# Attention in phases of two slots: six PSUM banks, waits bank by bank

## The chip, the cores and the metric

The kernel runs on one core of one Trainium2 chip. The time is the device time of an execution in microseconds. TensorE (PE) multiplies matrices, and its weight loads (PEld) are listed apart; ScalarE (ACT) computes the exponentials; VectorE (DVE) and GpSimd (POOL) add; SyncE (SP) issues the transfers.

## The reference

The input is x of 2 images, 256 channels and 64 × 64 positions. Two layers are applied, each to a group-normalised x, and each adds its result to x. The first is a state-space block with an MLP; the change does not touch it. The second is attention over the 4096 positions of each image with 8 heads of 32 channels:

```python
qkv = einsum('bchw,oc->bohw', x, qkv_w) + qkv_b          # q, k, v: 8 heads x 32 channels
attn_weights = softmax(einsum('bhci,bhcj->bhij', q, k) / sqrt(32), axis=-1)
out = einsum('bhij,bhcj->bhci', attn_weights, v)
```

All data are float32.

## The kernel before

The first layer (`mamba_stage`) runs until about 1995 us and also computes q, k and v of the first image. Then `attention` runs image 0, prepares q, k and v of image 1 (`prepare`, with `project` and `project_values`), and runs image 1. Logits are not shifted by their maximum; `range_t` collects the sums' ranges, and a slow general path runs at the end only if they are out of range.

An image is cut into 16 query tiles: 2 groups of four heads by 8 tiles of 512 positions. A query tile walks over 32 blocks of 128 keys. One block of one query tile is a *slot*: four logits (L1162), one per head, each with 128 keys on the partitions and 512 queries in a PSUM bank; two exponentials (L1175), each over the two banks of two heads; and four value matmuls (L1199), each 32 output channels wide, which accumulate into the tile `po` over the 32 slots. The logits are single matmuls, because q and k are stored as a high and a low part stacked over the partitions. The value matmuls are full float32, and each shows as two instructions.

The slots are taken by halves, of two heads each. The logits of a half fill one tile of two banks from a ring of three (`ps_s`, six banks), and one exponential of 1024 columns empties it. `PHASES` lists twenty phases of three half slots and two of two for each query tile. In every turn of `run`, ScalarE gets the exponentials of phase k, TensorE the values of phase k − 1 and then the logits of phase k + 1. Where a phase cuts a slot, the slot's values are made in two parts of 256 columns. The order of instructions on every engine is the order in which they are written (`manual_schedule`), and each engine works through its own in that order.

The softmax's denominators are sums of the exponentials over all keys. For heads 0 and 1 the exponentials go to a tile `chunk` that holds four slots side by side; every third slot VectorE sums the four in one reduction (`sum_chunk`, L1184) and writes the result into the first place of the next `chunk` (there are two buffers). The last block, number 31, goes to a tile `e`. For heads 2 and 3 they go to a tile `e` (five buffers of one slot's half), and GpSimd adds it to `acc_p` (L1230 to L1239); in some slots VectorE takes one of the two heads into `acc_2`, a PSUM bank (L1234, L1236). At a tile's end `finish` copies `po`, adds the parts up, and over the next slots lets TensorE sum over the partitions (L1257), takes reciprocals, scales, adds bias and residual, and stores. `Slots` spreads these steps: a `yield n` lets n slots pass. `end` does the same for the very last tile. `project` also stores through `chunk` buffers.

Of the kernel before, what the change touches and what calls it, by code (L numbers as in the profile page):

```python
# [29 lines left out]
def group_norm_scales(nc, small, psum_tile, stats, gmat, eps_t, out):  # L30
# [9 lines left out]
    yield  # L40
    ps = psum_tile()
    for k in range(KC):
        nc.tensor.matmul(ps[:, k : k + 1], lhsT=gmat, rhs=mv[k][:, 0:1], start=True, stop=True)
    for k in range(KC):
        nc.vector.tensor_copy(out[k][:, 0:1], ps[:, k : k + 1])

# [5 lines left out]
    yield 4  # L52
    ps = psum_tile()
    for k in range(KC):
        nc.tensor.matmul(ps[:, k : k + 1], lhsT=gmat, rhs=e[k][:, 1:2], start=True, stop=True)
    yield
# [5 lines left out]
class Slots:  # L62
# [10 lines left out]
    def run(self):  # L73
        for entry in list(self.waiting):
            if entry[0] <= self.now:
                try:
                    entry[0] = self.now + (next(entry[1]) or 1)
                except StopIteration:
                    self.waiting.remove(entry)
        self.now += 1  # L80

# [887 lines left out]
def attention(ctx, tc, stats, consts, w, outs, scratch, range_t):  # L969
# [18 lines left out]
    ps_s = ctx.enter_context(tc.tile_pool(name="l1pss", bufs=3, space=PSUM))  # L988
# [11 lines left out]
    ep = ctx.enter_context(tc.tile_pool(name="l1e", bufs=5))  # L1000
# [8 lines left out]
    def s_tile():  # L1009
        return ps_s.tile([P, 2, T], F32, name="s", tag="s")  # L1010
# [11 lines left out]
    def load_x(t):  # L1022
        if t >= NT:
            return
        if t < 2:

            if t == 0:
                xn["q"] = p2.tile([P, 4, T], F32R, name="q").bitcast(F32)
            xn[t] = xn["q"][:, KC * t : KC * t + KC, :]
        else:  # L1030
            xn[t] = ep.tile([P, KC, T], F32, name="e")
        nc.sync.dma_start(xn[t], scratch.image(1).rearrange("(k p) l -> p k l", p=P)[:, :, bass.ts(t, T)])
# [7 lines left out]
    def project(t, i):  # L1040


        pm = s_tile()
        for m in range(KC):
            for c in range(KC):
                nc.tensor.matmul(  # L1046
# [5 lines left out]
                )  # L1052
        halves = chunk().rearrange("p q h t k -> p q (h t k)").rearrange("p q (m t) -> p q m t", t=T)
        for m in range(KC):
            bias = b_qkv[:, i * KC + m : i * KC + m + 1]
            nc.scalar.activation(halves[:, 0, m, :].bitcast(F32R), pm[:, m, :], AF.Identity, bias=bias)
            nc.vector.scalar_tensor_tensor(
                halves[:, 1, m, :].bitcast(F32R), pm[:, m, :], bias, halves[:, 0, m, :], ALU.add, ALU.subtract
            )
            nc.sync.dma_start(scratch.qk[KG + m, i, t].rearrange("s c h t -> (c h) s t"), halves[:, :, m, :])  # L1060

    def project_values(t):
        pm = s_tile()
        flat = pm.rearrange("p a t -> p (a t)")
        for j in range(T // P):
            for c in range(KC):
                nc.tensor.matmul(
# [6 lines left out]
        nc.scalar.copy(v[:, bass.ts(t, T // P), :].rearrange("p s c -> p (s c)"), flat)  # L1074
# [24 lines left out]
    def image(b):  # L1099
# [44 lines left out]
        sizes = [3] * ((2 * NC - 4) // 3) + [2, 2]  # L1144
        bounds = [0, *itertools.accumulate(sizes * (KG * NT))]
        PHASES = [range(*ends) for ends in zip(bounds, bounds[1:])]
        SHARED = [c for c in range(8, NC) if c % 8 in (0, 2, 4, 5, 6)]
        todo = {}
        tiles = {}

        def logits(s, half):
            if s >= S:
                return
            i, c = divmod(s, NC)
            kt, kj = divmod(c * P, T)
            if half == 0:
                todo[s] = Slot()
                todo[s].s, todo[s].e = [], []
            ps = s_tile()
            for j in range(2):  # L1160
                h = 2 * half + j
                nc.tensor.matmul(  # L1162
                    ps[:, j, :], lhsT=keys[i // NT, kt][:, h, kj : kj + P], rhs=queries[i][:, h, :], start=True, stop=True
                )
            todo[s].s.append(ps)

        def exponentials(s, half):
            if half == 0 and s % NC < NC - 1:
                k = place(s % NC)
                first = s % NC == 0 or k == 1 and s % NC > 1  # L1170
                todo[s].chunk = (todo.pop("chunk", None) or chunk()) if first else todo[s - 1].chunk
                e = todo[s].chunk[:, k // 2, :, :, k % 2]
            else:
                e = ep.tile([P, 2, T], F32, name="e")
            nc.scalar.activation(e, todo[s].s[half], AF.Exp, scale=SCALE)  # L1175
            todo[s].e.append(e)
# [9 lines left out]
        def values(first, end):  # L1186

            u = first
            while u < end:
                s, half = divmod(u, 2)  # L1190
                i, c = divmod(s, NC)
                g = i // NT
                width = 2 if half == 0 and u + 1 < end else 1
                cols = slice(half * T // 2, (half + width) * T // 2)
                u += width
                if c == 0 and half == 0:
                    tiles[i].po = ps_o.tile([P, T], F32, name="po")
                for h in range(4):
                    nc.tensor.matmul(  # L1199
                        tiles[i].po[h * D : (h + 1) * D, cols],  # L1200
                        lhsT=v[:, c, g * P + h * D : g * P + (h + 1) * D],
                        rhs=todo[s].e[h // 2][:, h % 2, cols],
# [7 lines left out]
        def add_up(s):  # L1210
            i, c = divmod(s, NC)
            tile_ = tiles[i]
            eb = todo[s].e[1]
            if last(i) and c == NC - 1:
                return
            if last(i) and c == NC - 2:
                pass
            elif c == NC - 2:
                tile_.acc = p1.tile([P, 3, T], F32, name="acc_sb")
                sum_chunk(s, tile_.acc[:, 0:2].rearrange("p h t -> p (h t)"))  # L1220
            elif place(c) == 3:
                todo["chunk"] = chunk()
                sum_chunk(s, todo["chunk"].rearrange("p q h t k -> p q (h t) k")[:, 0, :, 0])
# [17 lines left out]
        def finish(i):  # L1241
# [4 lines left out]
            po = p1.tile([P, T], F32, name="po_sb")  # L1246
            nc.vector.tensor_copy(po, d.po)
            acc = d.acc
            nc.vector.tensor_add(acc[:, 2, :], d.acc_2, d.acc_p[:, 0, :])
            nc.vector.tensor_add(acc[:, 0:2, :], acc[:, 0:2, :], todo[i * NC + NC - 1].e[0])  # L1250
            res = p3.tile([P, T], F32, name="res")
            nc.sync.dma_start(res, x[g * P : (g + 1) * P, cols])
            yield 3
            ps = ps_2.tile([P, T], F32, name="sums_ps", tag="a2")
            for h in range(4):
                part = acc[:, h, :] if h < 3 else d.acc_p[:, 1, :]
# [5 lines left out]
            r = p1.tile([P, T], F32, name="r")  # L1262
# [9 lines left out]
            at = b * KG * NT + i  # L1272
            nc.vector.tensor_reduce(range_t[:, 0, at : at + 1], sums, AX.X, ALU.max)
            nc.vector.tensor_reduce(range_t[:, 1, at : at + 1], r, AX.X, ALU.max)

        def end():
# [6 lines left out]
            ps = s_tile()[:, 0, :]  # L1283
# [3 lines left out]
            terms = [[todo[S - 2].chunk[:, k // 2, h, :, k % 2] for k in range(4)] for h in range(2)]  # L1287
            terms += [[d.acc_p[:, 0, :], acc], [d.acc_p[:, 1, :]]]

            def sum_up(rounds):  # L1290
                for n in rounds:
                    for h in range(4):
                        n_ = n - 4 + len(terms[h])
                        if 0 <= n_:
                            part = terms[h][n_] if n_ < len(terms[h]) else todo[S - 1].e[h // 2][:, h % 2, :]
                            nc.tensor.matmul(
                                ps[h * D : (h + 1) * D, :], lhsT=ones, rhs=part, start=(n_ == 0), stop=(n == 4)
                            )

            sum_up(range(4))  # L1300
            yield
            sum_up([4])
            r = p1.tile([P, T], F32, name="r")
            for j in range(T // P):
                nc.vector.reciprocal(r[:, bass.ts(j, P)], ps[:, bass.ts(j, P)])
# [5 lines left out]
            nc.vector.tensor_reduce(range_t[:, 0, at : at + 1], ps, AX.X, ALU.max)  # L1311
            nc.vector.tensor_reduce(range_t[:, 1, at : at + 1], r, AX.X, ALU.max)

        def run():
            k = 0
            while k <= len(PHASES) or b == 1 and side.waiting:
                for p in PHASES[k] if k < len(PHASES) else ():
                    s, half = divmod(p, 2)
                    i, c = divmod(s, NC)
                    if half == 0:  # L1320
                        if c == 0:
                            tiles[i] = Slot()
                            load_queries(i + 1)
                        if i % NT == NT - 1 and i < KG * NT - 1 and c % (T // P) == 0:

                            load_keys(i // NT + 1, c * P // T)
                        if b == 1 and 1 <= i <= KG:
                            nc.sync.dma_start(scratch.v[b * KG + i - 1, :, c, :], v[:, c, (i - 1) * P : i * P])
                        if b == 0 and s == S - 24:
                            load_x(0)  # L1330
                            load_x(1)
                        if b == 0 and s == S - 14:
                            normalise(0)
                    if k > 0 or b == 0:
                        exponentials(s, half)
                    if half == 1:
                        add_up(s)
                if b == 0 and k == len(PHASES):
                    project(0, 1)
                turns = 1  # L1340
                if 0 < k <= len(PHASES):
                    units = PHASES[k - 1]
                    ending = end() if b == 1 and k == len(PHASES) else iter(())
                    next(ending, None)
                    values(units[0], units[-1] + 1)
                    next(ending, None)
                    turns = sum(u % 2 for u in units)
                    if (units[-1] + 1) % (2 * NC) == 0 and not last(units[-1] // (2 * NC)):
                        side.start(side.now, finish(units[-1] // (2 * NC)))
                for _ in range(turns):  # L1350
# [4 lines left out]
        def phase_logits(k):  # L1355
            for p in PHASES[k] if k < len(PHASES) else ():
# [203 lines left out]
```

## Time and profile before

| | us |
|---|---|
| median of 3 runs | 4287.08 (4286.70 to 4295.39) |
| the profiled execution | 4289.86 |
| its span | 4288.1 |
| one query tile in steady attention | 67.85 |

Costliest groups of attention (engine, what, count, mean of one in us):

| line | engine | what | count | mean |
|---|---|---|---|---|
| L1162 | PE | logits, 128x512 | 4096 | 0.415 |
| L1199 | PE | values, 512 and 256 columns | 10752 | 0.51 |
| L1175 | ACT | exponentials into `e`, 1024 columns | 1056 | 1.028 |
| L1175 | ACT | exponentials into `chunk`, 1024 columns | 992 | 1.126 |
| L1184 | DVE | sums of four slots | 319 | 4.41 |
| L1239 | POOL | additions of both heads | 479 | 2.432 |
| L1237 | POOL | additions of one head | 480 | 1.297 |

A record of TensorE or ScalarE begins before the one ahead of it has ended[...]. So the means above are longer than the steps from start to start. The value matmuls of four heads use different columns of the array and run side by side.

### The profile page before, as it was taken

To read this page: it belongs to the slowest core of one execution; us is meant where nothing else is said; L and a number is where in the kernel's file an instruction comes from. 1 tells how busy PE (TensorE), PEld (TensorE's weight loads), DVE (VectorE), ACT (ScalarE), POOL (GpSimd) and SP (SyncE) were. 2 spreads that over 40 slices of the span, in tenths; PEclk is the share of its full clock that TensorE was granted. 3 is DMA by queue.
4 is the path that set the end of the run, shared out by engine and by line. 5 is a ranking of instruction groups with operands and counts; after the bars stand their busy time and mean duration, and the time that the engine had idled before them with its cause. 6 is when DMAs were issued, how large, how long until landed. Compare 5 with 4: busy or idle time off the path is not lost.

```text
span 4288.1 us, 58982 instructions
## 1 busy us (share of the span) xinstructions
PE 4119.0 (96%) x21176; PEld 1802.7 (42%) x21176; DVE 3855.6 (90%) x3304; ACT 3729.2 (87%) x4983; POOL 3751.9 (87%) x1913
## 2 busy tenths in 40 slices
PE   6799999999999999988999999999999999999998
PEld 2233333333333343333444444444454444444443
DVE  6899999999999999994988989899849889898998
ACT  5789898999788888874999999999859999999997
POOL 3999999999899999994888988889728989888897
PEclk8899999999999999999999999999999999999999
DMA  6334333344444444447101040110181110401100
GB/s 212 105 114 130 113 113 126 129 133 133 150 144 163 154 141 142 142 167 168 34 24 28 18 106 18 28 30 21 40 262 46 40 28 18 106 18 28 30 21 9
DMA packets 172302, 389.58 MB, mean 91 GB/s; under 512 B 23392, under 2 KB 49760, under 8 KB 163808
## 3 DMA queue, kind: packets, MB, share of 16 engines
q1 hardware_dynamic: 171120, 383.37, 29.4%
q8 instruction: 168, 2.75, 0.3%
q10 hardware_dynamic: 880, 2.36, 0.3%
q14 instruction: 134, 1.10, 0.1%
HBM read 292.33 MB, written 93.32 MB: 90 GB/s over the span
## 4 chain that ended last, share of the span: by engine, by line
PE 82%; DVE 10%; ACT 3%; issue 2%; DMA 1%; POOL 1%; SPq 0%; DVEq 0%; POOLq 0%; ACTq 0%
PE s L1162 25%; PE po L1199 24%; PE mm L448 16%; DVE h L869 6%; PE y L901 4%; PE mm L688 4%; PE bn L448 2%; PE mm L647 2%; DVE bn L860 1%; PE s L1046 1%; PE y L899 1%; PE mm L684 1%; PE sums_ps L1257 1%; ACT da L853 1%; ACT L248 1%
## 5 line engine op out<-in xcount | busy, mean ns | idle before, releaser
L1184 DVE TENSOR_REDUCE chunk<-chunk 128x1024 f32<-128x4096 f32 x288 | 1269.9, 4409 | 169.5 <-ACT chunk L1175 168.2
L1239 POOL TENSOR_TENSOR acc_p<-acc_p,e 128x1024 f32<-128x1024 f32 x479 | 1165.1, 2432 | 121.2 <-ACT e L1175 96.6
L875 POOL TENSOR_TENSOR h<-h,c 128x1024 f32<-128x1024 f32 x512 | 1204.5, 2378 | 33.1 <-issue 15.7
L1162 PE MATMUL s<-q,k 128*128 128x512 f32 x4096 | 1155.0, 415 | 7.3 <-ACT chunk L1175 3.1
L1175 ACT ACTIVATE e<-s 128x1024 f32<-128x1024 f32 x1056 | 1081.8, 1028 | 91.4 <-PE s L1162 58.9
L1175 ACT ACTIVATE chunk<-s 128x1024 f32<-128x1024 f32 x992 | 1117.3, 1126 | 49.3 <-PE s L1162 22.5
L1199 PE MATMUL po<-chunk,v 128*32 128x512 f32 (+1 forms) x5248 | 1057.0, 521 | 0.0
L1199 PE MATMUL po<-e,v 128*32 128x512 f32 (+1 forms) x5504 | 1020.5, 500 | 4.2 <-ACT e L1175 4.2
L1162 PEld LDWEIGHTS s<-q,k 128*128 128x128 f32 x4096 | 713.9, 188 | 624.7 <-ACT e L1175 233.9
L853 ACT ACTIVATE da<-dt_rep,neg_a 128x512 f32<-128x512 f32 x1024 | 695.6, 702 | 107.9 <-DVE h L869 103.7
L1237 POOL TENSOR_TENSOR acc_p<-acc_p,e 128x512 f32<-128x512 f32 x480 | 622.3, 1297 | 95.5 <-ACT e L1175 65.7
L869 DVE TENSOR_TENSOR_SCAN h<-da,state,dbu 128x512 f32<-128x512 f32 x512 | 650.1, 1272 | 14.6 <-PE y L901 7.4
L869 DVE TENSOR_TENSOR_SCAN h<-da,state,bn 128x512 f32<-128x512 f32 x512 | 645.6, 1261 | 11.1 <-PE y L901 5.0
L864 POOL TENSOR_TENSOR dbu<-dtu_rep,b 128x1024 f32<-128x1024 f32 x176 | 418.0, 2375 | 18.8 <-issue 9.1
L448 PE MATMUL bn<-proj,pick 112*128 112x512 f32 x512 | 341.9, 669 | 89.1 <-DVE h L869 86.2
L248 ACT ACT_TABLE_LOAD x312 | 400.3, 1283 | 6.2 <-PEq L1550 0.7
L1199 PEld LDWEIGHTS po<-e,v 128*32 128x32 f32 x5504 | 251.6, 109 | 272.1 <-issue 105.3
L860 DVE TENSOR_TENSOR bn<-dtu_rep,bn 128x512 f32<-128x512 f32 x512 | 345.4, 677 | 18.0 <-PE bn L448 8.0
L1199 PEld LDWEIGHTS po<-chunk,v 128*32 128x32 f32 x5248 | 240.2, 108 | 251.2 <-issue 251.2
L1236 DVE TENSOR_TENSOR acc<-acc,e 128x512 f32<-128x512 f32 x448 | 309.5, 691 | 17.4 <-DVE acc L1236 0.5
L901 PE MATMUL y<-h,sum 128*32 128x512 f32 x2048 | 299.3, 613 | 6.9 <-POOL h L875 6.8
L448 PE MATMUL mm<-yn,w_in 128*128 128x512 f32 x512 | 255.2, 623 | 7.9 <-ACT yn L538 3.8
(163 smaller groups left out, 4182.9 us busy)
## 6 DMA issues: line engine op xcount, KB each, us to landing
dt_rep<-dt_dram SPq DMA_DIRECT2D x128, 512.0 KB, 5.0
dtu_rep<-dtu_dram SPq DMA_DIRECT2D x128, 512.0 KB, 5.3
k<-qk_dram SPq DMA_DIRECT2D x62, 512.0 KB, 7.6
q<-qk_dram SPq DMA_DIRECT2D x124, 256.0 KB, 4.8
b<-bc_dram SPq DMA_DIRECT2D x64, 256.0 KB, 3.1
c<-bc_dram SPq DMA_DIRECT2D x64, 256.0 KB, 3.8
dt_dram<-dt SPq DMA_DIRECT2D x64, 256.0 KB, 2.3
dtu_dram<-lw SPq DMA_DIRECT2D x64, 256.0 KB, 3.6
```

What stands on the lines that cost most here:

```text
L248: self.nc.scalar.preload_act_table_set(self.TABLES[task.table])
L448: nc.tensor.matmul(out, lhsT=lhsT, rhs=rhs, start=(i == 0), stop=(i == len(pairs) - 1))
L853: nc.scalar.activation(da[j].tile, dt.tile[:, j, :], AF.Exp, scale=scale)
L869: nc.vector.tensor_tensor_scan(h.tile[:, j, :], da[j].tile, dbu, initial, ALU.mult, ALU.add)
L875: nc.gpsimd.tensor_tensor(h.tile, h.tile, rows_c.tile.unsqueeze(1).to_broadcast([P, 2, T]), ALU.mult)
L901: nc.tensor.matmul(y.tile[j * PQ : (j + 1) * PQ, :], lhsT=sum4, rhs=pair[j // 2].h.tile[:, j % 2, :], start=False, stop=(qd == NQ - 1),)
L1162: nc.tensor.matmul(ps[:, j, :], lhsT=keys[i // NT, kt][:, h, kj : kj + P], rhs=queries[i][:, h, :], start=True, stop=True)
L1175: nc.scalar.activation(e, todo[s].s[half], AF.Exp, scale=SCALE)
L1184: nc.vector.tensor_reduce(out, terms, AX.XY, ALU.add)
L1199: nc.tensor.matmul(tiles[i].po[h * D : (h + 1) * D, cols], lhsT=v[:, c, g * P + h * D : g * P + (h + 1) * D], rhs=todo[s].e[h // 2][:, h % ...
L1237: nc.gpsimd.tensor_add(acc_p[:, 1, :], acc_p[:, 1, :], eb[:, 1, :])
L1239: nc.gpsimd.tensor_add(acc_p, acc_p, eb)
```

## The change

A phase is now always two whole slots, 16 phases a query tile. One PSUM tile `banks` of six banks is used bank by bank. The tile framework's own waits on it are turned off, and a class `Banks` records for each bank which instruction last wrote it and which read it, and adds just those waits.

The eight logits of a phase are issued in this order: heads 2 and 3 of the first slot into the pair `single`; heads 0 and 1 of the first slot into `first`; heads 0 and 1 of the second slot into `second`; then heads 2 and 3 of the second slot into `single` again. Before those last two, ScalarE is given two exponentials of one bank each, which empty `single`. Later come the exponentials of `first`, `second` and again `single`, two banks each. The pairs change roles from phase to phase. A tile `e` now holds heads 2 and 3 of both slots (three buffers of four banks' size).

Values are always made in full width. Block 31 goes to `chunk` like the others, so the last sum of four goes into a new `chunk`, and `finish` adds that one's two places. The steps of `finish` are spread differently, and the reciprocals overwrite the sums. In the group norm, a copy moves to ScalarE. `project` and `project_values` take their bank pairs in turn.

```diff
-        sizes = [3] * ((2 * NC - 4) // 3) + [2, 2]
-        bounds = [0, *itertools.accumulate(sizes * (KG * NT))]
-        PHASES = [range(*ends) for ends in zip(bounds, bounds[1:])]
+        K = S // 2
...
+    def s_banks(k):
+        return [2 * ((k + n) % 3) for n in range(3)]
...
+        def phase_logits(k):
+            if k >= K:
                 return
+            single, first, second = s_banks(k)
+            places = [(0, 2 + h, single + h) for h in range(2)]
+            places += [(0, h, first + h) for h in range(2)]
+            places += [(1, h, second + h) for h in range(2)]
+            places += [(1, 2 + h, single + h) for h in range(2)]
+            for n, (late, h, bank) in enumerate(places):
+                if n == 6:
+                    e = phases[k] = ep.tile([P, 4, T], F32, name="e")
+                    for j in range(2):
+                        exponential(e[:, j, :], single + j, 1)
+                i, c = divmod(2 * k + late, NC)
+                kt, kj = divmod(c * P, T)
+                mm = nc.tensor.matmul(
+                    banks[:, bank, :],
+                    lhsT=keys[i // NT, kt][:, h, kj : kj + P],
+                    rhs=queries[i][:, h, :],
+                    start=True,
+                    stop=True,
+                )
+                log.note(mm, "pe", [bank], True)
+
+        def exponential(e, bank, n):
+            ps = banks[:, bank, :] if n == 1 else banks[:, bank : bank + n, :]
+            done = nc.scalar.activation(e, ps, AF.Exp, scale=SCALE)
+            log.note(done, "act", range(bank, bank + n), False)
+
+        def exponentials(k):
+            single, first, second = s_banks(k)
+            e = phases.pop(k)
+            for late, pair in enumerate((first, second)):
+                s = 2 * k + late
+                c = s % NC
                 todo[s] = Slot()
...
+                terms = todo[s].chunk[:, at // 2, :, :, at % 2]
+                exponential(terms, pair, 2)
+                todo[s].e2 = e[:, 2 * late : 2 * late + 2, :]
+                todo[s].e = [terms[:, 0, :], terms[:, 1, :], e[:, 2 * late, :], e[:, 2 * late + 1, :]]
+                if at == 3 and not (last(s // NC) and c == NC - 2):
+                    todo["chunk"] = chunk()
+                    sum_chunk(s, todo["chunk"].rearrange("p q h t k -> p q (h t) k")[:, 0, :, 0])
+            exponential(e[:, 2:4, :], single, 2)
+            for s in (2 * k, 2 * k + 1):
+                add_up(s)
...
-        def values(first, end):
+        def values(k):
+            for s in (2 * k, 2 * k + 1):
...
                     nc.tensor.matmul(
-                        tiles[i].po[h * D : (h + 1) * D, cols],
+                        tiles[i].po[h * D : (h + 1) * D, :],
                         lhsT=v[:, c, g * P + h * D : g * P + (h + 1) * D],
-                        rhs=todo[s].e[h // 2][:, h % 2, cols],
+                        rhs=todo[s].e[h],
...
             po = p1.tile([P, T], F32, name="po_sb")
+            terms = [todo[i * NC + NC - 1].chunk[:, 0, :, :, k] for k in range(2)]
+            acc = p1.tile([P, 2, T], F32, name="acc_sb")
+            nc.vector.tensor_add(acc, terms[0], terms[1])
             nc.vector.tensor_copy(po, d.po)
-            acc = d.acc
-            nc.vector.tensor_add(acc[:, 2, :], d.acc_2, d.acc_p[:, 0, :])
-            nc.vector.tensor_add(acc[:, 0:2, :], acc[:, 0:2, :], todo[i * NC + NC - 1].e[0])
...
-            yield 3
+            yield 2
+            nc.vector.tensor_add(d.acc_p[:, 0, :], d.acc_p[:, 0, :], d.acc_2)
+            yield 4
```

## The prediction

> **What bounds the kernel now.** I read the page's busy shares, then the attention stage by windows, then the chain of waits through the end of one query tile, and last the timeline.
>
> ```profile
> PE 4119.0 (96%) x21176; PEld 1802.7 (42%) x21176; DVE 3855.6 (90%) x3304; ACT 3729.2 (87%) x4983; POOL 3751.9 (87%) x1913
> ```
>
> ```profile
> 2203.00:2336.00 133.00, 132.94 (x934) 62.36 (x926) 120.04 (x73) 124.57 (x127) 117.23 (x63) 1.00 0.10 25
> ```
>
> The second line is a window of steady attention: length, busy time of PE, PEld, DVE, ACT and POOL, granted clock, DMA. TensorE is busy 132.94 of 133 us at full clock; ScalarE 94%, VectorE 90%, GpSimd 88%. TensorE sets the pace. Attention lasts from 1995 us to the end, and by the starts of the copies of `po` one query tile (32 slots) takes 67.85 us, within 0.02 in 27 of 30 intervals. There are 32 tiles.
>
> ```profile
> 2408.59 1.53 PE po L1199 x13
> 2410.12 1.12 PE s L1162 x4
> 2411.24 1.05 PE po L1199 x6
> 2412.29 1.60 PE s L1162 x6
> 2413.89 0.99 PE po L1199 x8
> 2414.89 1.13 PE s L1162 x4
> 2416.01 0.03 issue
> 2416.04 0.73 PE s L1162 x2
> 2416.78 1.54 PE po L1199 x13
> 2418.32 1.60 PE s L1162 x6
> 2419.92 1.53 PE po L1199 x13
> 2421.45 0.86 PE sums_ps L1257 x8
> ```
>
> This is the chain around a tile's end (start, us, what). It alternates values (`po`) and logits (`s`), and beside them only the sums. A phase of three half slots is 1.60 of logits and 1.52 of values; a phase of one slot is 1.12 and 1.05 (0.99 where the keys' block 31 lies in `e` alone). The sums cost 0.86. The check: 20 × 3.12 + 2 × 1.12 + 1.05 + 0.99 + 0.86 = 67.54, and the wait at 2416.01 (six logits in 1.89 instead of 1.60) brings it to 67.83. So a tile is understood to 0.02 us.
>
> **TensorE's part of the change.** Logits: (1.60 − 1.12) / 2 = 0.24 each over a fixed 0.16; the single starts in the trace say 0.234 with 0.337 after the first and 0.328 from the last to the values. Eight take 0.337 + 6 × 0.234 + 0.328 = **2.07**. Values: of the whole slot inside a three-half phase, the passes follow at 0.43 (heads in `e`) and 0.46 (heads in `chunk`, which set the end):
>
> ```profile
> 2501.56 0.63 PE L1199 MATMUL po<-chunk,v 128*32 128x512 f32 x2
> 2502.02 0.64 PE L1199 MATMUL po<-chunk,v 128*32 128x512 f32 x2
> ```
>
> A second slot adds two such passes: 1.05 + 0.92 = **1.97**. A phase of two slots is then 4.04, and a tile 16 × 4.04 + 0.86 = 65.5 if TensorE never waits. Gain: 2.35 us a tile. Of it 1.7 are six phase changes less (each a fixed 0.16 of logits and 1.05 − 0.92 = 0.13 of values), 0.29 the wait at the tile's end, and the remaining 0.3 the half-width values (168 calls a tile become 128, each two instructions: 10752 down to 8192).
>
> The Trainium skill, "TensorE: Matmul & The Clock Gate", section Back-to-back issue gap, puts a lone 512-column matmul at N/2.4 + 2.5 = 216 ns; eight logits would be 0.14 us shorter than with the row's 0.234. The row has the 128-column weight load of every logit in it, so I take the row.
>
> **ScalarE's part.** Per two slots, four exponentials of 1024 columns become three and two of 512. Starts while it has work:
>
> ```profile
> 2505.34 1.03 ACT L1175 ACTIVATE e<-s 128x1024 f32<-128x1024 f32 x1
> 2506.47 1.11 ACT L1175 ACTIVATE chunk<-s 128x1024 f32<-128x1024 f32 x1
> 2507.47 1.01 ACT L1175 ACTIVATE e<-s 128x1024 f32<-128x1024 f32 x1
> 2508.37 1.11 ACT L1175 ACTIVATE chunk<-s 128x1024 f32<-128x1024 f32 x1
> ```
>
> From `chunk` to the next is 1.00, from `e` to the next 0.90. One of 512 columns out of PSUM without a bias operand is in the first layer:
>
> ```profile
> 1007.40 0.60 ACT L604 ACTIVATE lw<-mm 128x512 f32<-128x512 f32 x1
> 1007.89 0.59 ACT L605 ACTIVATE tmp<-mm 128x512 f32<-128x512 f32 x1
> 1008.37 0.20 ACT L872 COPY state<-h 128x2 f32<-128x2 f32 x1
> ```
>
> 0.48 to 0.49 from start to start, 0.60 long. So ScalarE goes from 2 × 1.00 + 2 × 0.90 = 3.80 to 2 × 1.00 + 0.90 + 2 × 0.49 = 3.88 per two slots: it still fits under 4.04, with 0.16 to spare. A rule of the skill speaks against it: "ScalarE: Activation LUTs", section Rules for kernel authors, budgets about 0.3 us per ACTIVATE plus 0.83 ns an element, which makes 5 × 0.3 + 4 × 0.85 = 4.90 of the new phase, and the kernel 512 × (4.90 − 4.04), some 440 us, longer than TensorE alone would have it. But it makes 4.60 of today's two slots, which the trace shows in 4.16 (2/3 of two phases of 3.12). Its fixed part is that of a lone instruction, and the back-to-back starts overlap it; I go by the starts.
>
> **The new wait.** The logits' last two matmuls of a phase go into the banks that its first two filled, so they wait for the two single exponentials of the same phase. In time from the phase's first logit: its record is 0.50 long, and ScalarE starts 0.04 to 0.10 after the end of the record it waits for (434 such starts): 0.57. The second single starts 0.49 later, 1.06, and ends at 1.66. TensorE's weight load follows the end by 0.05 (57 such starts): 1.71. Without a wait it would be at 1.51. What a late load costs shows before:
>
> ```profile
> 2076.76 0.30 PEld L1162 LDWEIGHTS s<-q,k 128*128 128x128 f32 x2 [0.46 <-ACT chunk L1175]
> 2077.43 0.11 PEld L1199 LDWEIGHTS po<-chunk,v 128*32 128x32 f32 x2 [0.36 <-issue]
> ```
>
> Two logits from a late load to the values take 0.67, so one takes 0.67 − 0.24 = 0.43. The values start at 1.71 + 0.43 = 2.14 instead of 2.07. Behind the waiting load on TensorE stand the values of the phase before, and nobody waits for those at once. ScalarE itself is then at 1.06 + 0.49 + 1.00 + 1.00 + 0.90 = 4.45 when the next single could start, and gets its logit at 4.11 + 0.57 = 4.68: it does not hold the loop. So a phase is 2.14 + 1.97 = 4.11. With start, pitch and length each at the short end (0.54, 0.48, 0.59) it is 4.06, at the long end (0.60, 0.50, 0.61) 4.16; without a wait 4.04. I take **4.10**.
>
> **The rest, by what covers it.** VectorE does the same reductions and additions; the sums of four now start alternately 5.1 and 7.1 us apart instead of 6.2. They take 4.41, and with the additions and reciprocals between, the longest backlog I get by hand is 1.3 us, while the exponential that needs the buffer comes 1.4 us after that; should it be late, ScalarE's 0.2 goes first, then TensorE stands. At a tile's end, from the first logit after it: the last sum of four runs to 3.0, one addition to 3.6, the new 1.22 us addition to 4.8, the copy of `po` (0.69, now behind it) to 5.5, and the next tile's values want the bank at 4.10 + 2.14 = 6.2. GpSimd's additions (2.43 and 1.30) are unchanged, and three `e` buffers of two slots give them over two phases. DMA orders of the odd slot go out one slot earlier on SP, behind nothing that is late. The two copies of the group norm (0.2 us) move to ScalarE at the start, and the steps of `finish` fall some slots later: under TensorE's work, and if not, 0.2 us once and up to 0.7 a tile. These I cost at zero. Not zero: the longer phases fill and drain once per image (about 0.5 + 1 us each), and the first projection of image 1 now needs a `chunk` buffer that the last values still read: its evacuation is about 3 us later, and that stage's chain runs through stores of such buffers. Together **+6 us**, between −4 (the start before also has such waits, which may fall better) and 10.
>
> **The sum.** A tile: 16 × 4.10 + 0.86 = 66.46, with the old 0.29 wait at the end taken as gone; 67.85 − 66.46 = 1.39, times 32 = 44 us. Less 6: 38. The profiled execution took 4289.9 with a span of 4288.1; the median run is 4287.1. 4288.1 − 38 = 4250 of span, and against the median 4249; I say **4250**. Each 0.01 us of a phase is 5.1 us of the whole.
>
> **The rivals.**
> 1. *The singles hide.* If the first start is early and TensorE takes the load ahead, the phase is 4.04: 75 us less 6, **4218**. For it: only 0.07 has to vanish. Against: the load visibly waits in the row above. With the ends at −4 it is 4208.
> 2. *No change worth the name.* At 4.17 a tile is 67.6, 9 us are gained and 6 lost: **4284**. The singles would need 0.06 more than I gave them.
> 3. *Slower: ScalarE's singles set the phase.* The place is the last logit's load. Instructions of 512 columns with a bias operand start 0.57 to 0.59 apart and last 0.69; were the singles so, the chain is 0.57 + 0.57 + 0.69 + 0.05 + 0.43 = 2.31, the phase 4.28, a tile 69.3: 48 us more, with the 6 **4341**. It decides from a phase of 4.19, 0.09 above mine. Against it: the exponentials here have a constant bias and keep 0.90 for 1024.
> That the change does not do what it says would show as phases of 4.16 with a wait for whole tiles; it is in case 2.
>
> **How the numbers follow.** My case has 0.53 (4230 to 4273), the hidden singles 0.18, no change 0.10, slower 0.19. The range reaches to 4208 below and to 4300 above, which leaves out most of case 3 and a little of case 1. About 0.2%, 8.6 us, is what a measurement tells from nothing: faster (below 4278.5) is my case, the hidden singles and 0.03 of no change, 0.74; same is the rest of no change and 0.01 of slower, 0.08; slower 0.18.
>
> **What would show it.** Chain of waits: values of 1.97 and logits of about 2.14 in turn, tiles of 66.5 us, 8192 instructions of values. ScalarE: singles of 0.60, 0.49 from the first to the second. PEld of `s`: a wait for `e` of about 0.2 once a phase. I am wrong if logits exceed 2.23, if the wait before them names DVE or POOL, or if the values of two slots are not 1.97.

## The result and the profile after

The changed kernel takes 4346.99 us (median; 4341.40 to 4354.22) against 4289.11 in the same comparison: a ratio of 1.0134, with a 95% interval of 1.0114 to 1.0153. It is slower by 58 us. The prediction was 4250 us (4208 to 4300), so it had the wrong sign.

The page's first lines and the share of each engine in the chain that ended last:

```profile
span 4352.4 us, 53806 instructions
PE 4133.8 (95%) x18620; PEld 1771.7 (41%) x18620; DVE 3873.0 (89%) x3301; ACT 3742.5 (86%) x5497; POOL 3738.5 (86%) x1912
...
PE 50%; DVE 35%; ACT 6%; issue 6%; DMA 2%; POOL 1%; SPq 0%; DVEq 0%; ACTq 0%; POOLq 0%
DVE chunk L1250 17%; PE mm L477 14%; PE s L1207 10%; PE po L1259 9%; DVE h L898 6%; PE mm L717 4%; DVE acc L1288 4%; PE y L930 4%; PE mm L676 2%; PE bn L477 2%; ACT chunk L1218 2%; DVE bn L889 2%; DVE sums L1320 1%; ACT e L1218 1%; ACT da L882 1%
```

The program has 5176 instructions fewer (58982 to 53806), nearly all of them TensorE's, as the change intends. But VectorE, which was 10% of the chain, is now 35% of it, and its sums of four (L1250) stand first of all lines. Its busy share has not risen: in the window of two tiles below (columns as before) it is 124.48 of 140 us, 89% against 90%.

```profile
2203.00:2343.00 140.00, 137.02 (x792) 61.91 (x788) 124.48 (x73) 128.47 (x161) 119.46 (x66) 1.00 0.09 23
```

TensorE, which had 0.06 us of idle time in 133, now has 3 in 140. A query tile takes 69.65 us instead of 67.85 by the copies of `po`, and in every fourth tile 70.9.

The chain of waits around a tile's end, from the last sum of one tile to the second phase of the next:

```profile
2216.51 4.33 DVE chunk L1250
...
2220.92 1.10 ACT chunk L1218
2222.02 0.04 issue
2222.06 0.74 PE s L1207 x2
2222.80 0.05 issue
2222.85 1.05 ACT e L1218
2223.90 0.04 issue
2223.94 1.46 PE s L1207 x4
2225.40 2.00 PE po L1259 x13
2227.40 2.16 PE s L1207 x8
2229.56 2.00 PE po L1259 x13
```

The last two lines are a regular phase: 2.16 of logits and 2.00 of values. Away from the tile's end a phase takes 4.13 to 4.20. That is above the predicted 4.10 and about its long end of 4.16. Before, two slots took 4.16 inside the phases of three halves, and 4.19 on the average of a whole tile without its sums, so the regular phases gain some 0.04 each on that average. The loss is in the lines above. ScalarE's first exponential into `chunk` of the new tile begins only when VectorE's last sum of the old tile has ended, and the logits wait for ScalarE in turn. ScalarE's own line at that place:

```profile
2217.38 1.09 ACT L1218 ACTIVATE e<-s 128x512 f32<-128x512 f32 x2 [0.15 <-issue]
2220.92 2.07 ACT L1218 ACTIVATE chunk<-s 128x1024 f32<-128x1024 f32 x2 [2.45 <-DVE chunk L1250]
```

It stands for 2.45 us. The two phases around a tile's end take about 5.3 us each instead of 4.15, which is 2.3 us a tile.

Why the buffer is not free follows from the code. There are two `chunk` buffers. Blocks 28 to 30 end one of them, A. Before, the last sum went to a tile `acc_sb` and block 31 to a tile `e`, so the next tile's block 0 took the other buffer, B, which was long free. Now the last sum and block 31 go into B, and block 0 needs A, which that very sum is still reading. Only one phase lies between.

### The profile page after: what moved, and what is told of

Read it like the earlier page. It is cut to its first block, busy times and chain, and to the rows that moved or that the text cites. A ratio compares the mean times of both kernels' runs of the same rounds, so it can differ in the third digit from the quotient of the medians.

```text
span 4352.4 us, 53806 instructions
## 1 busy us (share of the span) xinstructions
PE 4133.8 (95%) x18620; PEld 1771.7 (41%) x18620; DVE 3873.0 (89%) x3301; ACT 3742.5 (86%) x5497; POOL 3738.5 (86%) x1912
## 4 chain that ended last, share of the span: by engine, by line
PE 50%; DVE 35%; ACT 6%; issue 6%; DMA 2%; POOL 1%; SPq 0%; DVEq 0%; ACTq 0%; POOLq 0%
DVE chunk L1250 17%; PE mm L477 14%; PE s L1207 10%; PE po L1259 9%; DVE h L898 6%; PE mm L717 4%; DVE acc L1288 4%; PE y L930 4%; PE mm L676 2%; PE bn L477 2%; ACT chunk L1218 2%; DVE bn L889 2%; DVE sums L1320 1%; ACT e L1218 1%; ACT da L882 1%
## 5 line engine op out<-in xcount | busy, mean ns | idle before, releaser
L1250 DVE TENSOR_REDUCE chunk<-chunk 128x1024 f32<-128x4096 f32 x319 | 1404.6, 4403 | 262.6 <-ACT chunk L1218 262.2
L1291 POOL TENSOR_TENSOR acc_p<-acc_p,e 128x1024 f32<-128x1024 f32 x479 | 1152.1, 2405 | 158.3 <-ACT e L1218 91.8
L1207 PE MATMUL s<-q,k 128*128 128x512 f32 x4096 | 1172.0, 424 | 51.4 <-ACT chunk L1218 39.5
L1218 ACT ACTIVATE e<-s 128x512 f32<-128x512 f32 (+1 forms) x1536 | 1090.6, 751 | 106.2 <-PE s L1207 40.2
L1218 ACT ACTIVATE chunk<-s 128x1024 f32<-128x1024 f32 x1024 | 1095.8, 1139 | 80.2 <-DVE chunk L1250 72.9
L1259 PE MATMUL po<-chunk,v 128*32 128x512 f32 x4096 | 1065.4, 640 | 0.0
L1207 PEld LDWEIGHTS s<-q,k 128*128 128x128 f32 x4096 | 728.4, 189 | 796.7 <-ACT chunk L1218 480.8
L1259 PE MATMUL po<-e,v 128*32 128x512 f32 x4096 | 986.9, 603 | 0.0
L1259 PEld LDWEIGHTS po<-e,v 128*32 128x32 f32 x4096 | 194.7, 110 | 302.3 <-issue 302.0
L1259 PEld LDWEIGHTS po<-chunk,v 128*32 128x32 f32 x4096 | 193.2, 109 | 138.0 <-issue 137.3
```

The source lines that it names most:

```text
L1207: mm = nc.tensor.matmul(banks[:, bank, :], lhsT=keys[i // NT, kt][:, h, kj : kj + P], rhs=queries[i][:, h, :], start=True, stop=True,)
L1218: done = nc.scalar.activation(e, ps, AF.Exp, scale=SCALE)
L1250: nc.vector.tensor_reduce(out, terms, AX.XY, ALU.add)
L1259: nc.tensor.matmul(tiles[i].po[h * D : (h + 1) * D, :], lhsT=v[:, c, g * P + h * D : g * P + (h + 1) * D], rhs=todo[s].e[h], start=(c == 0 ...
L1291: nc.gpsimd.tensor_add(acc_p, acc_p, eb)
```

## The experiments

Three theories were set against each other. A: the ring of `chunk` buffers is one turn too far at each tile's end. B: VectorE's sums come unevenly, and its queue is late everywhere. C: the two single exponentials hold TensorE in every phase.

### Block 31 apart

The edit to the changed kernel (run `e1_block31_apart`; `...` marks lines left out here):

```diff
+                if c == NC - 1:
+                    terms = todo[s].e31 = p1.tile([P, 2, T], F32, name="e31")
...
+                if c == NC - 2 and not last(s // NC):
+                    tiles[s // NC].acc = p1.tile([P, 2, T], F32, name="acc_sb")
+                    sum_chunk(s, tiles[s // NC].acc.rearrange("p h t -> p (h t)"))
...
-            terms = [todo[i * NC + NC - 1].chunk[:, 0, :, :, k] for k in range(2)]
-            acc = p1.tile([P, 2, T], F32, name="acc_sb")
-            nc.vector.tensor_add(acc, terms[0], terms[1])
+            acc = d.acc
+            nc.vector.tensor_add(acc, acc, todo[i * NC + NC - 1].e31)
...
-            res = p3.tile([P, T], F32, name="res")
+            res = p1.tile([P, T], F32, name="res")
```

> The changed kernel with one part undone: block 31 of heads 0 and 1 goes to a tile of its own (4 KB, made room for by one buffer less of the residual), and the last sum of four goes to its own tile, so no third chunk buffer is wanted at a tile's end. Theory A (at a tile's end the first exponential of the next tile waits for the last sum, because the ring of two chunk buffers is one turn further): the two phases of 5.3 us around a tile's end fall to about 4.2, a tile from 69.65 to 67.3 us, the half-clock windows vanish, and the time falls by 32 x 2.3 + 7 x 1.25 = 82 us, 4347 to 4265. Theory B (VectorE's sums come unevenly, 5.1 and 7.1 us apart, and its queue is late all over the tile): the ring doesn't matter, 4347. Theory C (the two single exponentials hold TensorE in every phase): 4347, as every phase keeps its 4.15.

Measured: 4280.29 us, 0.9978 of the kernel before (0.9970 to 0.9986). A tile is 67.5 us, the longest phase at its end about 4.4, and all but one of the half-clock windows in steady attention are gone (stretches in which TensorE was granted half its clock; the last section shows them). That is 67 us off the changed kernel by this one part, and the sign of the whole change turns. Theory A holds, and B and C fall as the cause of the loss; 15 us less came off than expected, of which the fourth experiment finds 10.

### That part alone, in the kernel before

The edit (run `e2_before_block31_in_chunk`):

```diff
-            if half == 0 and s % NC < NC - 1:
+            if half == 0:
...
-            elif c == NC - 2:
-                tile_.acc = p1.tile([P, 3, T], F32, name="acc_sb")
-                sum_chunk(s, tile_.acc[:, 0:2].rearrange("p h t -> p (h t)"))
             elif place(c) == 3:
                 todo["chunk"] = chunk()
...
+            terms = [todo[i * NC + NC - 1].chunk[:, 0, :, :, k] for k in range(2)]
...
-            nc.vector.tensor_add(acc[:, 0:2, :], acc[:, 0:2, :], todo[i * NC + NC - 1].e[0])
+            nc.vector.tensor_add(acc[:, 0:2, :], terms[0], terms[1])
```

> The kernel before with only that part done: block 31 of heads 0 and 1 goes to a chunk and the last sum into a new chunk. Before, the last sum of a tile ran from 2070.0 to 2074.4 and the next tile's first exponential into a chunk began at 2073.7. Theory A: that exponential has to wait some 0.75 us for the sum, a tile is 68.6 instead of 67.85, the whole 4289 + 24 = 4313. Theories B and C: no change, 4289.

Measured: 4364.36 us, 1.0176 (1.0159 to 1.0193), 74 us more. The direction is A's, the size is three times what I expected: a tile is 70.33, 2.5 us longer and not 0.75. The next tile's first exponential into a `chunk` waits for the last sum by more than twice the expected time:

```profile
2212.98 1.09 ACT L1175 ACTIVATE chunk<-s 128x1024 f32<-128x1024 f32 x1 [1.66 <-DVE chunk L1184]
```

VectorE's instructions at that kernel's tile end show that the last sum began late:

```profile
2202.75 4.41 DVE L1184 TENSOR_REDUCE chunk<-chunk 128x1024 f32<-128x4096 f32 x1
2207.08 1.49 DVE L1233 TENSOR_TENSOR acc<-acc,e 128x512 f32<-128x512 f32 x2
2208.48 4.41 DVE L1184 TENSOR_REDUCE chunk<-chunk 128x1024 f32<-128x4096 f32 x1
2212.81 0.69 DVE L1233 TENSOR_TENSOR acc<-acc,e 128x512 f32<-128x512 f32 x1
...
2220.15 4.42 DVE L1184 TENSOR_REDUCE chunk<-chunk 128x1024 f32<-128x4096 f32 x1 [4.22 <-ACT chunk L1175]
```

The same two places in the kernel before, the last sum of a tile and the first of the next:

```profile
2137.90 4.42 DVE L1184 TENSOR_REDUCE acc_sb<-chunk 128x1024 f32<-128x4096 f32 x1 [0.43 <-ACT chunk L1175]
2148.73 4.42 DVE L1184 TENSOR_REDUCE chunk<-chunk 128x1024 f32<-128x4096 f32 x1 [2.78 <-ACT chunk L1175]
```

In both kernels the sums near the end follow one another with no pause, some 5.7 us apart, though three slots take 6.24: VectorE is catching up. Before, it had caught up at the last sum and waited 0.43 us for the exponential; here it has not. And it stands at the start of every tile, because a first sum needs four blocks of the new tile: 2.78 us before, 4.22 here. So the wait seems to close a loop: ScalarE waits for VectorE's last sum, VectorE then waits longer for ScalarE's first four blocks, and carries that lag to the next last sum. I tested this in the changed kernel below.

The lag has a second source. The step of `finish` that adds bias and residual takes four times as long here as before (shortest, median and longest in ns, of the kernel before and of this one):

```profile
L1270 DVE SCALAR_TENSOR_TENSOR res<-po_sb,b_qkv,res x31: 740/742/2774, 2112.0 to 4240.0; 128x512 f32<-128x512 f32 x31
L1268 DVE SCALAR_TENSOR_TENSOR res<-po_sb,b_qkv,res x31: 745/2955/2989, 2110.6 to 4315.8; 128x512 f32<-128x512 f32 x31
```

That is 2.2 us more of VectorE's time in 30 of 31 tiles, and the page has VectorE busy for 3919.9 us instead of 3855.6. The last section shows what lengthens it, an addition of GpSimd that runs at the same time. How much of the 2.5 us a tile is the loop and how much this step is not separated here.

### No wait for the singles

The edit to the kernel with block 31 apart is one line (run `e3_apart_no_single_wait`). This kernel leaves out the second slot's logits of heads 0 and 1, which are overwritten, so it only shows what the wait costs:

```diff
-            places += [(1, 2 + h, single + h) for h in range(2)]
+            places += [(1, 2 + h, second + h) for h in range(2)]
```

> As e1_block31_apart, but the last two logits of a phase go into the pair of the second slot's heads 0 and 1 (over what these hold), so they don't wait for the single exponentials; heads 2 and 3 of the second slot take the logits of the first. As many matmuls and exponentials as before. Theory C, and the predicted chain of singles: the logits of a phase fall from 2.16 to 2.07, the phase from 4.15 to 4.04, against e1_block31_apart 512 x 0.11 = 56 us less, about 4209. If ScalarE's own load or VectorE sets the phase instead: no change against e1_block31_apart.

Measured: 4344.81 us, 1.0136 (1.0119 to 1.0153): 65 us slower than with the wait. Yet the logits of a phase fell to 2.07, to the hundredth what the prediction's sum has without the wait, and the regular phase to 4.05 to 4.08. TensorE's waits on VectorE over 14 tiles of this kernel, and of the one with block 31 apart (us in total, times, longest):

```profile
PE po L1264 <- DVE po_sb L1306: 35.9, 13, 2.9
```

```profile
PE po L1264 <- DVE po_sb L1306: 2.0, 9, 0.3
```

At a tile's end the phase takes 6.8 to 8.4 us: the new tile's values wait for the copy of `po`, which stands behind the last sum and the addition of block 31. That addition is not 1.22 us long here:

```profile
2212.15 2.39 POOL L1287 TENSOR_TENSOR acc_p<-e 128x1024 f32<-128x1024 f32 x1 [1.87 <-ACT e L1218]
2212.41 3.22 DVE L1305 TENSOR_TENSOR acc_sb<-acc_sb,e 128x1024 f32<-128x1024 f32 x1
```

With the wait for the singles it kept its 1.22 us in all but one tile. It began just ahead of GpSimd's addition there, and that one took the longer time:

```profile
2215.81 1.22 DVE L1305 TENSOR_TENSOR acc_sb<-acc_sb,e 128x1024 f32<-128x1024 f32 x1
2215.83 3.47 POOL L1287 TENSOR_TENSOR acc_p<-e 128x1024 f32<-128x1024 f32 x1 [1.78 <-ACT e L1218]
```

So the wait for the singles had hidden VectorE's lateness. A part of the 65 us is the clock: the waits of 2.7 to 2.9 us brought half-clock windows in about every second tile; those tiles take 70.6 to 71.0 us, and most others 69.2 to 69.4.

### The copy of `po` first

The edit to the kernel with block 31 apart (run `e4_apart_po_first`):

```diff
+            nc.vector.tensor_copy(po, d.po)
             nc.vector.tensor_add(acc, acc, todo[i * NC + NC - 1].e31)
-            nc.vector.tensor_copy(po, d.po)
```

> As e1_block31_apart, with the copy of po ahead of the 1.22 us addition again, as in the kernel before. If VectorE's lateness at the tile's end (the last sum began 1.1 us after its last exponential) also keeps the next tile's values from their bank, a tile is up to 0.5 us shorter than in e1_block31_apart, 15 us in all; if not, the two are the same.

Measured: 4270.46 us, 0.9958 (0.9941 to 0.9974), 10 us less than with block 31 apart alone. A tile is 67.2, and the phase at its end 4.14 like all others. This kernel leaves nothing out and is faster than the kernel before and the changed one, and TensorE is 80% of its chain (82% before the change). The chain through a tile's end:

```profile
2220.64 1.98 PE po L1264 x14
2222.62 2.16 PE s L1207 x8
2224.78 1.99 PE po L1264 x13
2226.77 0.86 PE sums_ps L1315 x8
```

### The copy first and no wait for the singles

The two edits above together, in the kernel with block 31 apart (run `e5_po_first_no_single_wait`). It leaves out the same logits.

> As e4_apart_po_first, with the last two logits of a phase in the second slot's pair again (over what it holds), so that they don't wait for the singles; heads 2 and 3 of the second slot take the first slot's logits. In e3_apart_no_single_wait the regular phases fell to 4.05 to 4.08, but the values of a new tile waited up to 3.3 us for the copy of po. Theory D (there only the place of that copy behind the addition cost it): with the copy first the tile is about 16 x 4.06 + 0.86 = 65.8 and the time 4270 - 32 x 1.35 = 4227. Theory E (with shorter phases VectorE's work of some 62 us a tile, with its idle time at the tile's start, becomes the bound): a tile of 67 us or more, 4270 or above.

Measured: 4241.10 us, 0.9886 (0.9869 to 0.9902). A tile is 66.47, a regular phase 4.06. Theory D holds in the main: the place of the copy had cost the 104 us between this kernel and the one with the addition first, the half-clock windows included. The time is 14 us above D's 4227, since one phase in the middle of every tile takes about 4.8. There ScalarE waits for a sum of VectorE, which stands behind the residual step:

```profile
2248.74 1.62 DVE L1330 SCALAR_TENSOR_TENSOR res<-po_sb,b_qkv,res 128x512 f32<-128x512 f32 x1
2255.37 1.11 ACT L1218 ACTIVATE chunk<-s 128x1024 f32<-128x1024 f32 x1 [0.97 <-DVE chunk L1255]
```

In the kernel before, the residual step took 0.74 us. The wait for the singles is worth 4270 − 4241 = 29 us here, 0.06 us a phase. The regular phases gain 0.08 to 0.09, and the long phase takes some of it back.

### Fewer additions on VectorE

In the changed kernel itself, to test the loop (run `e6_fewer_vector_adds`):

```diff
-        SHARED = [c for c in range(8, NC) if c % 8 in (0, 2, 4, 5, 6)]
+        SHARED = [c for c in range(8, NC) if c % 8 in (0, 2, 4, 5, 6) and c not in (16, 18)]
```

> The changed kernel, with VectorE's additions into acc_2 of blocks 16 and 18 given to GpSimd (two of 14 a tile, 0.60 to 0.70 us each on VectorE, 1.1 more each on GpSimd, in the middle of the tile). Theory F (the wait at a tile's end closes a loop: ScalarE waits for the last sum, VectorE then stands until four blocks of the next tile are there, and drags that lag through the whole tile to the next last sum): the lag is smaller by what VectorE is spared, a tile 69.65 - 1.3 = 68.35, the time 4347 - 42 = 4305, some 8 less if the half-clock windows go. Theory G (the wait is only the last sum's own 4.4 us after its exponential): the middle of the tile doesn't matter, 4347.

Measured: 4318.08 us, 1.0068 (1.0051 to 1.0085): 29 us less than the changed kernel, and a tile of 68.67. Two additions in the middle of a tile shorten it by 1.0 us, some 0.9 of them at its end, twelve blocks and more later. That is theory F, and G falls. But VectorE was spared more than the two additions, because here its residual step no longer meets an addition of GpSimd (the changed kernel and this one, as above):

```profile
L1326 DVE SCALAR_TENSOR_TENSOR res<-po_sb,b_qkv,res x31: 736/1609/1623, 2125.4 to 4312.7; 128x512 f32<-128x512 f32 x31
L1326 DVE SCALAR_TENSOR_TENSOR res<-po_sb,b_qkv,res x31: 732/735/1050, 2123.4 to 4273.3; 128x512 f32<-128x512 f32 x31
```

So the run shows that VectorE's load in the middle of a tile sets the wait at its end; it does not say which of the two savings did it. F's 4305 was not reached, and the chain of this kernel, with ScalarE's waits over 14 tiles (us in total, times, longest), shows what is late next:

```profile
2215.78 1.08 PE po L1259 x6
2216.85 0.02 issue
2216.88 1.13 ACT chunk L1218
2218.00 0.04 issue
2218.05 0.75 PE s L1207 x2
```

```profile
ACT chunk L1218 <- PE po L1259: 23.2, 14, 1.7
```

The first exponential of the new tile now waits for the *values*: the value matmuls of block 30 read buffer A too, and they stand behind the eight logits of the phase. So A has two late readers, VectorE's sum and TensorE's values. The second alone costs 68.67 − 67.2 = 1.5 us a tile (67.2 is the kernel with the copy first, where neither is met), and VectorE's lag another 1.0.

### One pair for the two singles

The edit to the kernel with the copy first (run `e7_pair_for_singles`):

```diff
-                    for j in range(2):
-                        exponential(e[:, j, :], single + j, 1)
+                    exponential(e[:, 0:2, :], single, 2)
```

> As e4_apart_po_first, but one exponential over two banks in place of the two singles. By the prediction's chain it starts 0.09 after the second logit's record (0.34 + 0.39 + 0.09 = 0.82), lasts 1.00, the load follows at 1.87, and two late logits take 0.67 to the values: 2.54 instead of 2.16, a phase 4.52 instead of 4.14, 4270 + 512 x 0.38 = 4465. If ScalarE's load per phase counts more than this chain (3.80 instead of 3.88), the phase stays near 4.14 or falls.

Measured: 4478.44 us, 1.0435 (1.0417 to 1.0452). A phase takes 4.57, 0.05 more than the chain said. The load of the seventh logit waits:

```profile
2245.47 1.23 PEld L1206 LDWEIGHTS s<-q,k 128*128 128x128 f32 x6 [0.91 <-ACT chunk L1217]
2247.38 0.30 PEld L1206 LDWEIGHTS s<-q,k 128*128 128x128 f32 x2 [0.68 <-ACT e L1217]
```

The prediction's way of costing this wait, from the first logit through ScalarE and back to the last load, is thus right at three sizes: no wait, singles, pair. The singles are worth 208 us against the pair, although ScalarE has more to do with them.

## Why the prediction was wrong

**Right: TensorE's part.** Logits without a wait 2.07 (measured 2.07), with it 2.14 (2.16), values of two slots 1.97 (1.98 to 2.00), no stall at the tile's end (the kernel with the copy first has none). ScalarE's singles are 0.59 long and 0.49 apart, and the last load waits 0.27 on them once a phase:

```profile
2101.84 0.19 PEld L1207 LDWEIGHTS s<-q,k 128*128 128x128 f32 x1 [0.27 <-ACT e L1218]
2102.27 0.11 PEld L1259 LDWEIGHTS po<-chunk,v 128*32 128x32 f32 x2 [0.25 <-issue]
```

The phase came to 4.15 and not 4.10 because ScalarE starts 0.09 to 0.10 after the first logit's record, at the end of the 0.04 to 0.10 that I had averaged, and the values are 0.02 longer. Over 512 phases that is 25 us of the expected 44; the kernel with the copy first shows what this part of the change brings, 19 us.

**Failed: the step "The rest, by what covers it".** It costs VectorE's side at zero. I followed the `chunk` buffers within a tile, and I even saw that the first projection of image 1 "now needs a `chunk` buffer that the last values still read", but charged it once, at the images' boundary. The same is true at every tile's end, where the next tile's first exponential takes that buffer, with the last sum as a second reader. In its place the runs show 69.65 − 67.2 = 2.45 us a tile, 78 us in all: 1.5 for the values' reading, 1.0 for VectorE's lag. Moving block 31 stands in that step only as "the new 1.22 us addition", and alone it costs the kernel before 74 us.

**Mis-sized in the same step: VectorE's queue.** I wrote that VectorE does the same reductions and additions. The instructions are the same, but the residual step, which moved with the rest of `finish`, takes 1.61 us instead of 0.74 in the changed kernel. The backlog that I put at 1.3 us against 1.4 us to spare is 0.1 to 0.2 us late in the middle of most tiles there, and 0.8 to 1.2 in the kernel with the copy first and no wait for the singles. I gave the copy of `po` 0.7 us to spare at the tile's end. With the ring mended it is about 0.3 us late (10 us in all), and with shorter phases up to 2.9, where the addition ahead of it took 3.2 us: VectorE's queue has less slack at that place than the sum of its instructions says.

**The ends.** I took 6 us off for them; 32 tiles of 67.2 give 21 us, and the kernel with the copy first gained 19. They cost about 2.

**The rivals.** The measured 4347 lies next to the slower rival's 4341, but that is chance: its mechanism was the singles at 4.28 a phase, and they gave 4.15. The prediction's own marks were the right ones: "I am wrong if logits exceed 2.23, if the wait before them names DVE or POOL". At a tile's end the logits take 3.3, and the wait before them leads through one exponential of ScalarE to DVE.

**Settled, and open.** Shown: block 31's place decides the sign, by undoing it and by doing it alone; that VectorE's work in the middle of a tile sets the wait at its end, by sparing it work; the price of the singles, at three sizes. Read from the traces, without an edit that tests it alone: that GpSimd's additions lengthen VectorE's residual step, and that this makes the long phase in the middle of a tile. Open: how VectorE's 1.0 us a tile divides between the loop and that step, and whether a third `chunk` buffer would do as well; no run has one.

## What to carry to other kernels

When a change moves one item into a ring of buffers, count the ring's turns over the whole period, its seam included: the wait appears where the next period takes a buffer one turn early, and every reader of that buffer has to be asked, not only the one that frees it in the steady part. An engine at 90% has little to give back after a forced pause: a wait that lengthens its pause at the seam (here from 2.78 to 4.22 us) makes it late for the rest of the period, and can so renew itself. Steps that a change only shifts can come to cost more, where they now meet another engine's work; compare their durations too. And a wait that costs little can hide a worse one; take both away before saying what either is worth.

## What was not expected of the hardware

**VectorE and GpSimd hold each other up.** Two kinds of VectorE's steps are lengthened where they begin while a GpSimd addition runs: the residual step (from 0.74 to 1.6 or 2.95 us) and the addition of block 31 (from 1.22 to 3.2). Both read two operands from SBUF. In every such case of all the runs they end the same time after GpSimd's addition, to 0.01 us, whenever they began: 0.55 us for the 512 columns of the one and 1.08 for the 1024 of the other. So they look as if they waited for it. Where VectorE's addition began first, GpSimd's took 3.47 us instead of 2.39. The sums of four, which read one operand, and the additions into `acc_2`, which lies in PSUM, kept their 4.4 and 0.69 us beside a running GpSimd. No run was made to test this by itself.

**Half the clock after short pauses.** The tiles of 70.9 us come from TensorE's clock. In one of them, two windows of 4 us at a tile's end (columns as before; the clock is the third from the end):

```profile
2150.00:2154.00 4.00, 2.47 (x7) 1.19 (x8) 2.24 (x3) 4.00 (x6) 0.96 (x1) 0.94 0.10 30
2154.00:2158.00 4.00, 4.00 (x19) 1.16 (x19) 2.05 (x1) 2.82 (x3) 3.84 (x3) 0.63 0.01 4
```

After pauses of 1.16, 0.22 and 0.16 us within one tile's end, the granted clock was half for 3.4 us, and the values' passes came 0.85 us apart instead of 0.43; that phase of values took 2.98 us, and the tile 1.2 more. It happened in every fourth tile, though the pauses are nearly alike in all of them. The steps between these half-clock windows are 279.9 us, 82 times their length of 3.41. The Trainium skill ("TensorE: Matmul & The Clock Gate", "What's actually happening") says that TensorE's activity is judged over free-running windows of 3413 ns. The traces agree: in all nine, every change of the clock during attention lies on a grid of 3.413 us. The same section says that the clock falls after an idle window, and the section "HAM oscillation — how this bites in real kernels" has the rule that no idle gap should exceed some 3.4 us; here 1.54 us in three pieces were enough, so the measurement decides. On that grid, the seven windows ahead of a half clock hold 1.43 to 1.56 us of TensorE's pauses, and no other window of steady attention in this kernel holds more than 1.37. So the place of the grid decides which tile is hit: a tile's pauses fall mostly into one window only in every fourth. In the kernel with no wait for the singles the border lies elsewhere: windows with 2.09 us and more were followed by half the clock, windows with up to 2.04 were not. What else counts than the pauses stays open. With the shorter pauses of the kernel with fewer additions (0.29, 0.22, 0.17) there were none in steady attention. Seven such tiles are some 9 us of the 58; an eighth window falls into the last tile.
